# A Mamba-2 mixer with a ternary FFN: another order in the mixer's first ten steps and in step 64, and other turns for the side work of the FFN

## The chip, the cores and the metric

The kernel runs on one core of a Trainium2 chip, in one launch. The metric is the device time of the launch in microseconds (us). TensorE (PE), VectorE (DVE), ScalarE (ACT), GpSimd (POOL) and SyncE (SP) each run their own instructions in the order in which the program gives them; they wait for each other through semaphores. SP and POOL issue the transfers (DMAs).

## The reference

T = 4 x 256 = 1024 rows of 512 values. After a layer norm they go two ways: through a gated FFN with ternary weights, and through a Mamba-2 mixer (128 heads of 64, 8 groups, state 128). The output is x + mixer x silu(FFN). Cut to what matters:

```python
xn = layernorm(x)                                   # (4, 256, 512)
# mixer
zxbcdt = xn @ in_proj_w.T                           # gate 8192 | x 8192, B 1024, C 1024 | dt 128
xBC = silu(causal_conv(xBC, conv_w, 4 taps) + conv_b)
dt = softplus(dt + dt_bias);  Adt = -exp(A_log) * dt
# per head, with B, C shared by 16 heads, i >= j:
y[i] = sum_j (C[i] . B[j]) * exp(sum_{j<k<=i} Adt[k]) * dt[j] * x[j] + D * x[i]
# (the reference sums this in chunks of 32 with states)
y = y * silu(gate)
y = y * rsqrt(mean over group of y^2 + eps) * norm_w
s = y @ out_proj_w.T                                # 8192 -> 512
# FFN
hidden = silu(xn @ gate_w.T) * (xn @ up_w.T)        # 512 -> 1792, weights -1, 0, 1 times a scale
g = silu(hidden @ down_w.T)
return x + s * g
```

## The kernel before

**Two stages and an end.** `front` computes the layer norm and the FFN, and beside it what the mixer needs: dt and the decay rows, the B and C projections and the scores C.B of the 8 groups. Then the mixer runs in CT = 64 steps of 128 channels (two heads), and two more, 64 and 65, in which only older work is finished. At the end the last group's out-projection is done batch by batch (4 batches) and joined with the FFN's result.

**Products in seven parts.** Both projections of the mixer are done with 7 block products instead of 8 (a Strassen-like form). `product` (L173) issues two matmuls of a 128 x 128 block of weights by 512 columns. The weights are used as blocks a11, a12, a22 and as sums s1, s2, s3, s4, the activations as x11, x21, x22 and t1 to t4. `combine_w` (L142 to L146) makes the sums of weights on DVE, four additions a step. For the first EARLY = 7 steps the sums are made beside the FFN (`early_pieces`), stored to DRAM and loaded in the step. `out_first` (L701) is the same form of the out-projection, with its left sums (L681 to L684) and 7 products P0 to P6 of four matmuls; behind each product `leave` (L756) scales a result on ACT into `sa` or `sb`, which POOL's transfers (L889, L890, L892) add to `acc` in DRAM. The pool of sa and sb has one buffer each.

**FFN steps.** There are 28 (2 halves by 14 tiles). Each has a gate product, an up product, the down product of the step before, and three turns, in which `pieces` (84 turns and more) does its side work: `first_pieces` (the layer norm of tiles 4 to 7 and the activations' sums), from turn 5 on `dt_pieces` (thirteen pieces, two turns each, with exp and ln on ACT), at turns 11 + 8g `bc_pieces(g)` (the B and C projections of a group: products, three taps on DVE at L181, the last tap on ACT at L177, silu at L186, scores at L438), and from turn 26 on the sums for the mixer's first steps. The gate's silu is L520, the rounding rest of the hidden values is `hl` (L545). Copies of products to `cpad` and `xpad` are L404.

**A mixer step i.** The projection's seven products give the gate `gT` and the channels `xpad`; conv and silu give `xT`. In the same step the channels of i - 1 are worked on: the decay matrices m (two heads; rows broadcast from DRAM, `decay_scan` L592 on DVE, `decay_exp` L595 on ACT) are multiplied by the group's scores (`meet`, L598 and L599 on DVE), xT is transposed on PE (L604) and multiplied by dt into `v` (`values_0` L612 for the first block, `values_1` L621 for the second), and `y_products` (L645) sums y in PSUM (begun by `y_begin`, L631 on ACT). Channels i - 2 are gated in `y_gate` (L652) and written to DRAM; their squares are added to `sqacc` (L863, a transfer of POOL). From step 10 on each step also does 4 or 3 products of the out-projection of a group finished earlier.

**What sets the order.** The schedule is manual: each engine runs the instructions as the Python code emits them. For i < LEAD = 6 the silu of step i is put off to step i + 1, with the first exp behind it; from LEAD on both stand at the end of step i. The lines of a step that the change touches:

```python
                product(px, a11, x11, True)
                nc.scalar.copy(pz, px)                          # L782
            if old and i - 1 < LEAD:
                conv_silu(i - 1, xTs[i - 1])
                decay_exp(ms[i - 1][0])
            if old:
                decay_exp(ms[i - 1][1])
            if here:
                product(pq, s1, t1, True)
                product(px, s2, t2, False)
                nc.scalar.copy(gT[:, HALF:], px)                # L791
```

In step 64 nothing is projected (`here` is false). It gates channels 62, treats channels 63, and does P0 to P3 of an out-projection, P4 to P6 of which follow in step 65.

Of the kernel before, what the change touches and what calls it, by code (L numbers as in the profile page):

```python
# [61 lines left out]
G = 8  # L62
# [12 lines left out]
LEAD = 6  # L75
EARLY = 7
# [5 lines left out]
def mixer_ffn(ctx: ExitStack, tc: tile.TileContext, x, in_w, conv_w, conv_b, dt_bias, a_log, d_col,  # L82
# [23 lines left out]
    scp = main.enter_context(tc.tile_pool(name="scp", bufs=1))  # L106
# [82 lines left out]
    def front(pre, one_of, fp, f2, hp, wq):  # L189
# [136 lines left out]
        def dt_ln():  # L326
            nc.scalar.activation(ln, u, AF.Ln)
            nc.vector.scalar_tensor_tensor(e, u, 1.0, e, ALU.subtract, ALU.subtract)
            nc.scalar.activation(u, ln, AF.Exp, scale=-1.0)
# [43 lines left out]
        def first_pieces():  # L373
            yield
            for t in range(4, NT):
                keep(t, ln_tile(t))
                yield
            for n in range(4):
                combine_x(n)
                if n == 2:  # L380
                    held["a"] = combine_w(held.pop("w"))
                yield

        def dt_pieces():
            for piece in (lambda: dt_project(0), lambda: dt_project(1), dt_exp, dt_ln, dt_softplus,
                          dt_adt, dt_sums, dt_rows, lambda: transpose_heads(dt[:, 0], dth, 0),
                          lambda: transpose_heads(dt[:, 1], dth, 1),
                          lambda: transpose_heads(adt0, adt, 0), tail_sums, tail):
                piece()
                yield  # L390
                yield

        def bc_pieces(g):
# [7 lines left out]
            for a, b, to in ((a11, x11, cpad_h[0]), (s2, t2, cpad_h[1]), (s3, t3, bpad_h[1]),  # L401
                             (a22, t4, bpad_h[0])):
                product(px, a, b, a is a11)
                nc.scalar.copy(to, by_batch(px))  # L404
                yield
# [15 lines left out]
            s = scp.tile([P, 3, KT // 2, P], F32, name="s")  # L421
            held["a"] = factors(w, s)
            sums = combine_to(s[:, 0], s[:, 1], s[:, 2], blocks(w)[2], w)
            next(sums)
            yield
            next(sums)
            conv_taps(i_b, bT, xpad, (0,))
            conv_silu(i_c, cT)
            yield
            conv_taps(i_b, bT, xpad, (1, 2))  # L430
# [16 lines left out]
        def early_pieces():  # L447
            for n in range(EARLY):
                w = wq.tile([P, 2, KT, P], F32, name="wq")
                for m, i in enumerate((n + 1, CT + n + 1)):  # L450
                    nc.sync.dma_start(w[:, m], in_w[i])
                for _ in range(4):
                    yield
                s = wq.tile([P, 4, KT // 2, P], F32, name="sq")
                yield from combine_to(s[:, 0], s[:, 1], s[:, 2], s[:, 3], w)
                nc.sync.dma_start(early[n], s)
                yield

        def all_pieces():

            turn, chains = 0, [first_pieces()]
            later = []
            while chains or later or turn < 11 + 8 * G:
                if turn == 5:
                    later.append(dt_pieces())
                if turn >= 11 and (turn - 11) % 8 == 0 and (turn - 11) // 8 < G:
                    chains.insert(0, bc_pieces((turn - 11) // 8))
                if turn == 26:
                    later.append(early_pieces())
                if turn > 11 and (turn - 11) % 8 == 4 and len(chains) > 1:  # L470
# [39 lines left out]
        for t in range(4, NT):  # L510
            ln_stats(t)
        ln_std(4, 4)
        nc.vector.reciprocal(rstd[:, 4:], rstd[:, 4:])
# [54 lines left out]
    yap = main.enter_context(tc.tile_pool(name="yap", bufs=2, reuse_waits="tile"))  # L568
# [172 lines left out]
    with tc.manual_schedule():  # L741
# [3 lines left out]
        sqacc, rs, ya, outs = None, None, None, None  # L745
        for i in range(CT + 2):
# [4 lines left out]
            sums = []  # L751
# [5 lines left out]

            if i + 1 <= EARLY:
# [24 lines left out]
            if old and i - 1 < LEAD:  # L783
                conv_silu(i - 1, xTs[i - 1])
                decay_exp(ms[i - 1][0])
            if old:
                decay_exp(ms[i - 1][1])
            if here:
                product(pq, s1, t1, True)
                product(px, s2, t2, False)  # L790
                nc.scalar.copy(gT[:, HALF:], px)  # L791
                if i:
                    decay_scan(ms[i][0])
# [24 lines left out]
            if og >= 0 and on % 2 == 0:  # L818
                ob, ya = on // 2, nxt
                left, sums = left_factors(ya)  # L820
                for make in sums:
                    make()
# [13 lines left out]
            if here:  # L836
                product(px, a22, t4, False)
                nc.scalar.copy(xpad_h[0], by_batch(px))
                product(pq, s4, x22, False)
                nc.vector.tensor_add(gT[:, HALF:], gT[:, HALF:], pq)  # L840
            if old:
# [6 lines left out]
            if og >= 0:  # L848
                if on % 2 == 0:
                    sa = osp.tile([P, NC, HID], F32, name="sa")  # L850
                    sb = osp.tile([P, 3, HH], F32, name="sb")
                    outs = out_first(left, rights[og], leave)
                for n in range(4 - on % 2):
                    next(outs)
                    if here and n == 1:
                        nc.scalar.activation(gT[:, HALF:], gT[:, HALF:], AF.Silu)
            elif here:
                nc.scalar.activation(gT[:, HALF:], gT[:, HALF:], AF.Silu)
# [7 lines left out]
            if here:  # L866
# [12 lines left out]
                if i == 0:  # L879
                    decay_scan(ms[i][0])  # L880
                decay_scan(ms[i][1])
# [13 lines left out]
            elif i == CT:  # L895
                nxt = load_gated(G - 1, 0, PER_G - 1)
# [20 lines left out]
        for b in range(NB):  # L917
# [14 lines left out]
            sums = []  # L932
            for n, _ in enumerate(out_first(left, rights[G - 1], leave_last)):
                if n == 4:
# [4 lines left out]
            if b + 1 < NB:  # L939
                left, sums = left_factors(yas[b + 1])  # L940
                for make in sums:
                    make()
# [50 lines left out]
```

## Time and profile before

| | |
|---|---|
| median of 3 runs | 1818.32 us (1817.26 to 1818.66) |
| profiled execution | 1815.84 us, of which the core's span is 1814.1 |
| mean granted clock of TensorE | 0.993 |
| a mixer step without out-projection, step 5 (410.55 to 428.33) | 17.78 us |
| a step with `combine_w`, step 8 (465.16 to 484.21) | 19.05 us |
| P0 of the four last batches starts | 1756.81, 1769.03, 1782.60, 1796.16 |

All times inside the kernel are microseconds from the start of the span, for one profiled execution. L12 is line 12 of the kernel before. In a line of the timeline the columns are start, duration, engine, line, operation, output and inputs, count, and in brackets the idle time of the engine before it, with what ended it. PEclk is the clock that TensorE was granted, 1.00 being full speed. Matmul ends are modelled, so that a busy PE is not PE at its peak.

### The profile page before, as it was taken

To read this page: it belongs to the slowest core of one execution; us is meant where nothing else is said; L and a number is where in the kernel's file an instruction comes from. 1 tells how busy PE (TensorE), PEld (TensorE's weight loads), DVE (VectorE), ACT (ScalarE), POOL (GpSimd) and SP (SyncE) were. 2 spreads that over 40 slices of the span, in tenths; PEclk is the share of its full clock that TensorE was granted. 3 is DMA by queue.
4 is the path that set the end of the run, shared out by engine and by line. 5 is a ranking of instruction groups with operands and counts; after the bars stand their busy time and mean duration, and the time that the engine had idled before them with its cause. 6 is when DMAs were issued, how large, how long until landed. Compare 5 with 4: busy or idle time off the path is not lost.

```text
span 1814.1 us, 22556 instructions
## 1 busy us (share of the span) xinstructions
PE 1744.4 (96%) x8494; PEld 1116.3 (62%) x8494; DVE 1448.0 (80%) x1739; ACT 1069.8 (59%) x1420; POOL 194.7 (11%) x235
## 2 busy tenths in 40 slices
PE   8999999899899999999999999999999999999988
PEld 6566666444456666666666666666666666666676
DVE  5557665689898888888888888888888888888866
ACT  3443333576666666666666666666666666666630
POOL 2212221000000000111011101110111011101110
PEclk9999999999999999999999999999999999999989
DMA  5134543557646665766676667665766676667665
GB/s 203 64 134 174 180 139 108 192 188 243 200 161 204 197 201 181 205 197 196 188 206 197 201 182 205 197 203 181 205 196 201 183 205 194 192 193 204 177 183 168
DMA packets 161739, 337.05 MB, mean 186 GB/s; under 512 B 15072, under 2 KB 54752, under 8 KB 161632
## 3 DMA queue, kind: packets, MB, share of 16 engines
q1 hardware_dynamic: 139120, 283.19, 44.7%
q0 software_dynamic: 22512, 52.44, 16.6%
q8 instruction: 67, 1.10, 0.2%
q14 instruction: 40, 0.33, 0.1%
HBM read 232.55 MB, written 74.19 MB: 169 GB/s over the span
## 4 chain that ended last, share of the span: by engine, by line
PE 85%; DVE 6%; ACT 5%; DMA 1%; issue 1%; SPq 0%; DVEq 0%; ACTq 0%
PE px L173 27%; PE po L701 21%; PE pq L173 13%; PE py L645 9%; PE pz L173 6%; PE pp L283 4%; PE pf L291 2%; ACT xpad L803 2%; PE tp L604 1%; PE pg L438 1%; DMA wd_i<-in_down_t 1%; ACT m L595 1%; PE pv L663 1%; DVE xT L181 1%; DVE cT L181 1%
## 5 line engine op out<-in xcount | busy, mean ns | idle before, releaser
L173 PE MATMUL px<-xc,w 128*128 128x512 f32 x576 | 280.1, 609 | 26.3 <-ACT xpad L803 15.7
L592 DVE TENSOR_TENSOR_SCAN m<-m,after 128x1024 f32<-128x1024 f32 x128 | 291.8, 2281 | 0.0
L181 DVE SCALAR_TENSOR_TENSOR xT<-xpad,cw,xT 128x1024 f32<-128x1024 f32 x192 | 246.1, 1282 | 4.6
L173 PEld LDWEIGHTS px<-xc,w 128*128 128x128 f32 x576 | 103.8, 190 | 147.1 <-issue 97.2
L701 PE MATMUL po<-wo,ya 128*128 128x256 f32 x768 | 178.1, 382 | 0.0
L645 PE MATMUL py<-m,v 128*64 128x128 f32 x2048 | 160.6, 276 | 5.3 <-DVE v L621 5.3
L598 DVE TENSOR_TENSOR m<-m,gm 128x1024 f32<-128x1024 f32 x128 | 154.7, 1209 | 6.8 <-ACT m L595 6.8
L701 PEld LDWEIGHTS po<-wo,ya 128*128 128x128 f32 x768 | 142.6, 192 | 17.4 <-issue 0.2
L863 POOL DMA_DIRECT2D sqacc<-sq x55 | 48.3, 878 | 955.0 <-ACT sq L815 955.0
L173 PE MATMUL px<-xc,s 128*128 128x512 f32 x288 | 136.0, 594 | 6.6 <-ACT pz L782 6.3
L173 PE MATMUL px<-xnT,w 128*128 128x512 f32 x288 | 141.8, 614 | 0.0
L173 PE MATMUL pq<-xc,s 128*128 128x512 f32 x288 | 135.4, 592 | 1.4 <-DMA s<-early 1.4
L173 PE MATMUL pq<-xnT,s 128*128 128x512 f32 x288 | 135.7, 593 | 0.5 <-DVE xpad L827 0.4
L595 ACT ACTIVATE m<-m 128x1024 f32<-128x1024 f32 x128 | 134.8, 1057 | 1.7 <-DVE m L592 0.9
L173 PE MATMUL pz<-xnT,w 128*128 128x512 f32 x288 | 135.3, 592 | 0.0
L645 PEld LDWEIGHTS py<-m,v 128*64 128x64 f32 x2048 | 116.9, 137 | 27.3 <-issue 19.8
L701 PE MATMUL po<-tw,sy 128*128 128x256 f32 x512 | 116.9, 380 | 2.8 <-DVE sy L681 1.5
L840 DVE TENSOR_TENSOR gT<-gT,pq 128x512 f32<-128x512 f32 x64 | 43.9, 687 | 83.5 <-PE pq L173 83.5
L604 PEld LDWEIGHTS tp<-ident,xT 128*128 128x128 f32 x512 | 64.1, 141 | 74.9 <-issue 74.9
L827 DVE TENSOR_TENSOR xpad<-xpad,pq 128x512 f32<-128x512 f32 x64 | 43.8, 684 | 83.3 <-ACT xpad L803 83.1
L701 PEld LDWEIGHTS po<-tw,sy 128*128 128x128 f32 x512 | 96.8, 190 | 18.4 <-DVE m L922 2.8
L652 DVE TENSOR_TENSOR yg<-py,gT 128x512 f32<-128x512 f32 x128 | 83.8, 678 | 27.6 <-PE py L645 27.6
(168 smaller groups left out, 3072.3 us busy)
## 6 DMA issues: line engine op xcount, KB each, us to landing
m<-rows SPq DMA_DIRECT2D x128, 512.0 KB, 6.1
w<-in_in_w SPq DMA_DIRECT2D x137, 256.0 KB, 6.6
mo<-rows SPq DMA_DIRECT2D x128, 256.0 KB, 7.0
gated<-yg SPq DMA_DIRECT2D x64, 512.0 KB, 8.2
ya<-gated SPq DMA_DIRECT2D x31, 1024.0 KB, 7.0
sqacc<-sq POOLq DMA_DIRECT2D x55, 512.0 KB, 5.4
wo<-in_out_w SPq DMA_DIRECT2D x64, 256.0 KB, 6.9
acc<-sa POOLq DMA_DIRECT2D x24, 512.0 KB, 5.9
```

The lines of the kernel that those rows point to most:

```text
L173: nc.tensor.matmul(pp, a[:, k, :], b[:, k, :], start=start and k == 0, stop=k == KT // 2 - 1, skip_group_check=not start)
L181: nc.vector.scalar_tensor_tensor(xT, xpad[:, :, k:k + L], cw[:, i, k:k + 1], xT, ALU.mult, ALU.add)
L283: nc.tensor.matmul(pp, w[:, k * P:(k + 1) * P], part[:, k, :], start=(k == 0 and part is xh), stop=(k == KT - 1 and part is xl))
L592: nc.vector.tensor_tensor_scan(m, m, after, 0.0, ALU.add, ALU.mult)
L595: nc.scalar.activation(m, m, AF.Exp)
L598: nc.vector.tensor_mul(m, m, gm[:, 0:T])
L604: nc.tensor.transpose(tp[:, b, :], xT[:, b, c * P:(c + 1) * P], ident)
L645: nc.tensor.matmul(py[d, q * P:(q + 1) * P], v[:, b, h, :], m, start=False, stop=stop, skip_group_check=True)
L652: nc.vector.tensor_mul(yg[:, 2 * i:2 * i + 2, :], ps[i], by_batch(gT[:, i * HALF:(i + 1) * HALF]))
L701: nc.tensor.matmul(po, a[:, k, :], b[:, k, :], start=start and k == 0, stop=k == HG - 1, skip_group_check=not start)
L840: nc.vector.tensor_add(gT[:, HALF:], gT[:, HALF:], pq)
L863: nc.gpsimd.dma_start(sqacc, sq, accum_op=ALU.add)
```

## The change

- LEAD becomes 9 and EARLY 11. For steps 8 to 11 the sums of weights are thus made beside the FFN too, and loaded.
- Beside the FFN: statistics of tiles 4 to 7 move from before the first FFN step into the first turns; the pieces of dt get turn counts of their own, start a turn later, and the inverse is split off; the sums of the next group's weights stand behind products s2 and s3; the B taps are a turn earlier; the early sums start at turn 20 and take five turns each instead of seven.
- In the first steps of the mixer the second exp stands behind the gT copy (in step 1 there is no exp), the values of block 1 ahead of the gT addition on DVE as long as there is no out-projection, and step 0 ends with both exps.
- In step 64 and 65 the left sums and the products of the out-projection open the step.
- Batches 0 and 1 of the last group are loaded in step 64; in the last stage the left sums of batch b + 1 are made one by one from the fourth product of batch b on.
- Pools `scp` and `yap` get a buffer more each.

```diff
-LEAD = 6
-EARLY = 7
+LEAD = 9
+EARLY = 11
...
-    scp = main.enter_context(tc.tile_pool(name="scp", bufs=1))
+    scp = main.enter_context(tc.tile_pool(name="scp", bufs=2))
...
             nc.vector.scalar_tensor_tensor(e, u, 1.0, e, ALU.subtract, ALU.subtract)
+
+        def dt_inverse():
             nc.scalar.activation(u, ln, AF.Exp, scale=-1.0)
...
         def first_pieces():
+            for t in range(4, NT):
+                ln_stats(t)
+                if t % 2:
+                    yield
+            ln_std(4, 4)
+            nc.vector.reciprocal(rstd[:, 4:], rstd[:, 4:])
             yield
...
-            for piece in (lambda: dt_project(0), lambda: dt_project(1), dt_exp, dt_ln, dt_softplus,
-                          dt_adt, dt_sums, dt_rows, lambda: transpose_heads(dt[:, 0], dth, 0),
-                          lambda: transpose_heads(dt[:, 1], dth, 1),
-                          lambda: transpose_heads(adt0, adt, 0), tail_sums, tail):
+            for piece, turns in ((lambda: dt_project(0), 2), (lambda: dt_project(1), 1),
+                                 (dt_exp, 3), (dt_ln, 3), (dt_inverse, 1), (dt_softplus, 1),
+                                 (dt_adt, 2), (dt_sums, 2), (dt_rows, 1),
+                                 (lambda: transpose_heads(dt[:, 0], dth, 0), 1),
+                                 (lambda: transpose_heads(dt[:, 1], dth, 1), 1),
+                                 (lambda: transpose_heads(adt0, adt, 0), 1), (tail_sums, 2),
+                                 (tail, 1)):
                 piece()
-                yield
-                yield
+                for _ in range(turns):
+                    yield
...
                 nc.scalar.copy(to, by_batch(px))
+                if a is s2:
+                    s = scp.tile([P, 3, KT // 2, P], F32, name="s")
+                    held["a"] = factors(w, s)
+                    sums = combine_to(s[:, 0], s[:, 1], s[:, 2], blocks(w)[2], w)
+                if a is not a11:
+                    next(sums, None)
                 yield
...
             conv_taps(i_c, cT, cpad, (2,))
-            s = scp.tile([P, 3, KT // 2, P], F32, name="s")
-            held["a"] = factors(w, s)
-            sums = combine_to(s[:, 0], s[:, 1], s[:, 2], blocks(w)[2], w)
-            next(sums)
+            conv_taps(i_b, bT, xpad, (0,))
             yield
-            next(sums)
-            conv_taps(i_b, bT, xpad, (0,))
             conv_silu(i_c, cT)
+            conv_taps(i_b, bT, xpad, (1, 2))
             yield
-            conv_taps(i_b, bT, xpad, (1, 2))
             yield
...
-                for _ in range(4):
+                for _ in range(2):
                     yield
...
-                if turn == 5:
+                if turn == 6:
                     later.append(dt_pieces())
...
-                if turn == 26:
+                if turn == 20:
                     later.append(early_pieces())
...
-    yap = main.enter_context(tc.tile_pool(name="yap", bufs=2, reuse_waits="tile"))
+    yap = main.enter_context(tc.tile_pool(name="yap", bufs=3, reuse_waits="tile"))
...
+            if not here:
+                left_sums()
+                project_out(lambda: None)
...
-            if old and i - 1 < LEAD:
+            lead = old and i - 1 < LEAD
+            if lead:
                 conv_silu(i - 1, xTs[i - 1])
-                decay_exp(ms[i - 1][0])
-            if old:
+                if i > 1:
+                    decay_exp(ms[i - 1][0])
+            elif old:
                 decay_exp(ms[i - 1][1])
             if here:
                 product(pq, s1, t1, True)
                 product(px, s2, t2, False)
                 nc.scalar.copy(gT[:, HALF:], px)
+                if lead and i > 1:
+                    decay_exp(ms[i - 1][1])
...
                 nc.scalar.copy(xpad_h[0], by_batch(px))
+                if i == 0:
+                    decay_scan(ms[i][0])
+                    decay_scan(ms[i][1])
                 product(pq, s4, x22, False)
+            if old and og < 0:
+                vs.append(values_1(i - 1, xTs[i - 1]))
+            if here:
                 nc.vector.tensor_add(gT[:, HALF:], gT[:, HALF:], pq)
-            if old:
+            if old and og >= 0:
                 vs.append(values_1(i - 1, xTs[i - 1]))
...
-                if i == 0:
-                    decay_scan(ms[i][0])
-                decay_scan(ms[i][1])
+                if i:
+                    decay_scan(ms[i][1])
+                else:
+                    decay_exp(ms[i][0])
+                    decay_exp(ms[i][1])
...
-                nxt = load_gated(G - 1, 0, PER_G - 1)
+                yas = {b: load_gated(G - 1, b, PER_G - 1) for b in range(2)}
...
-        yas = {0: nxt, 1: load_gated(G - 1, 1)}
-        last = yas[0][:, PER_G - 1, :]
-        nc.vector.tensor_copy(last, yg[:, 0, :])
+        yas[2] = load_gated(G - 1, 2)
+        for b in range(2):
+            nc.vector.tensor_copy(yas[b][:, PER_G - 1, :], yg[:, b, :])
...
             for n, _ in enumerate(out_first(left, rights[G - 1], leave_last)):
+                if n == 3 and b + 1 < NB:
+                    ahead, sums = left_factors(yas[b + 1])
+                if n >= 3 and b + 1 < NB:
+                    sums.pop(0)()
...
-            if b + 1 < NB:
-                left, sums = left_factors(yas[b + 1])
-                for make in sums:
-                    make()
+            left = ahead
             if b + 2 < NB:
-                yas[b + 2] = load_gated(G - 1, b + 2)
                 whole[b + 2] = fetch(b + 2)
+            if b + 3 < NB:
+                yas[b + 3] = load_gated(G - 1, b + 3)
```

`left_sums` and `project_out` hold the lines that made the left sums and called `out_first` before, unchanged; in steps 0 to 63 they are called at the old places.

More of the change, by code (lines that the diff above doesn't have):

```diff
@@ L509, in front @@
             keep(t, tps[t])
[L510 to L513, printed above, removed]
         last = None
@@ L744, in mixer_ffn @@
         xTs, gTs, yps, wos, rights, toms = {}, {}, {}, {}, {}, {}
-        sqacc, rs, ya, outs = None, None, None, None
+        sqacc = rs = ya = outs = left = nxt = ob = sa = sb = None
         for i in range(CT + 2):
@@ L750, in mixer_ffn @@
             wg, wn = og + 1, on
-            sums = []
             def leave(po, row, col, layer):
@@ L756, in leave, with project_out, left_sums @@
                 nc.scalar.mul(to, po, rs[:, 2 * ob + row:2 * ob + row + 1])
+            def project_out(between):
+                nonlocal sa, sb, outs
+                if on % 2 == 0:
+                    sa = osp.tile([P, NC, HID], F32, name="sa")
+                    sb = osp.tile([P, 3, HH], F32, name="sb")
+                    outs = out_first(left, rights[og], leave)
+                for n in range(4 - on % 2):
+                    next(outs)
+                    if n == 1:
+                        between()
+            def left_sums():
+                nonlocal ob, ya, left
+                if og >= 0 and on % 2 == 0:
+                    ob, ya = on // 2, nxt
+                    left, sums = left_factors(ya)
+                    for make in sums:
+                        make()
+            if not here:
+                left_sums()
+                project_out(lambda: None)
             if i + 1 <= EARLY:
@@ L815, in mixer_ffn @@
                     nc.scalar.activation(sq, yf, AF.Square)
-            if og >= 0 and on % 2 == 0:
-                ob, ya = on // 2, nxt
-                left, sums = left_factors(ya)
-                for make in sums:
-                    make()
+            if here:
+                left_sums()
             if wg >= 0 and wn == PER_G - 1:
@@ L838, in mixer_ffn @@
                 nc.scalar.copy(xpad_h[0], by_batch(px))
+                if i == 0:
+                    decay_scan(ms[i][0])
+                    decay_scan(ms[i][1])
                 product(pq, s4, x22, False)
+            if old and og < 0:
+                vs.append(values_1(i - 1, xTs[i - 1]))
+            if here:
                 nc.vector.tensor_add(gT[:, HALF:], gT[:, HALF:], pq)
-            if old:
+            if old and og >= 0:
                 vs.append(values_1(i - 1, xTs[i - 1]))
@@ L847, in mixer_ffn @@
                 nc.scalar.activation(gT[:, 0:HALF], pz, AF.Silu)
[L848 to L858, printed above, removed]
+                if og >= 0:
+                    project_out(lambda: nc.scalar.activation(gT[:, HALF:], gT[:, HALF:], AF.Silu))
+                else:
+                    nc.scalar.activation(gT[:, HALF:], gT[:, HALF:], AF.Silu)
             if old:
@@ L878, in mixer_ffn @@
                     ms[i + 1] = load_rows(i + 1)
-                if i == 0:
-                    decay_scan(ms[i][0])
-                decay_scan(ms[i][1])
+                if i:
+                    decay_scan(ms[i][1])
+                else:
+                    decay_exp(ms[i][0])
+                    decay_exp(ms[i][1])
             if here and i >= LEAD:
@@ L930, in end @@
                 nc.sync.dma_start(out[t * P:(t + 1) * P, cols], to)
-            sums = []
             for n, _ in enumerate(out_first(left, rights[G - 1], leave_last)):
+                if n == 3 and b + 1 < NB:
+                    ahead, sums = left_factors(yas[b + 1])
+                if n >= 3 and b + 1 < NB:
+                    sums.pop(0)()
                 if n == 4:
@@ L938, in mixer_ffn @@
             end(1, slice(0, HH))
-            if b + 1 < NB:
-                left, sums = left_factors(yas[b + 1])
-                for make in sums:
-                    make()
+            left = ahead
             if b + 2 < NB:
-                yas[b + 2] = load_gated(G - 1, b + 2)
                 whole[b + 2] = fetch(b + 2)
+            if b + 3 < NB:
+                yas[b + 3] = load_gated(G - 1, b + 3)
     main.close()
```

## The prediction

> **What bounds the kernel now.** I read the page's busy line first, then TensorE's table of waits, then the timeline around the long waits, and last the granted clock where they end.
>
> ```profile
> PE 1744.4 (96%) x8494; PEld 1116.3 (62%) x8494; DVE 1448.0 (80%) x1739; ACT 1069.8 (59%) x1420; POOL 194.7 (11%) x235
> PE   8999999899899999999999999999999999999988
> ```
>
> TensorE (PE) is busy 1744.4 of 1814.1 us, so at most 70 us can be won by a new order, and the change removes no matmul. These 70 us, by releaser (microseconds in all, times, longest):
>
> ```profile
> PE px L173 <- ACT xpad L803: 15.7, 64, 0.7
> PE tp L604 <- DVE v L612: 8.2, 1, 8.2
> PE tp L257 <- DVE xt L252: 6.8, 4, 3.2
> PE px L173 <- ACT pz L782: 6.3, 4, 1.6
> PE py L645 <- DVE v L621: 5.3, 9, 0.7
> PE px L173 <- ACT cpad L404: 5.3, 3, 3.3
> PE px L173 <- ACT gT L791: 3.8, 6, 2.0
> ```
>
> The xpad wait (0.24 us in each of 64 steps) stays. The others lie where the change works: L257, L404 beside the FFN, L791 in steps 1 to 6, L782 in steps 7 to 10, L621 in steps 1 to 9, L612 in step 64. A wait costs more than itself when the clock falls (timeline, idle time in brackets):
>
> ```profile
> 59.96 3.78 PE L173 MATMUL px<-xc,w 128*128 128x512 f32 x4 [3.27 <-ACT cpad L404]
> 307.43 1.51 PE L438 MATMUL pg<-cT,bT 128*128 128x128 f32 x8 [3.01 <-ACT bT L186]
> 346.59 1.98 PE L173 MATMUL px<-xc,w 128*128 128x512 f32 x4 [2.02 <-ACT gT L791]
> ```
>
> Behind the 3.27 gap four matmuls take 3.78 us, behind the 2.02 gap 1.98. In 2 us windows from each start the clock column is 0.50, 0.67 and 1.00. Work at reduced clock cost 2.75 us after the first and about 1.9 after the second (longer durations summed against the same shapes at full clock).
>
> **A, start of the FFN: +1.1 us** (plus is gain). LayerNorm statistics of tiles 4 to 7 leave VectorE's way ahead of FFN step 0. Replaying VectorE's order with its own durations, the two gaps of 3.19 and 1.46 become about 3.1 and 1.4; the same work is reached at 35.7 instead of 36.85. The moved statistics land in FFN turns 0 to 2, where VectorE is about half busy; without that cover they would delay the first hl by up to 1 us.
>
> **B, dt beside the FFN: +5.0.** The 3.27 wait came from ScalarE's run of tables:
>
> ```profile
> 54.00 1.06 ACT L327 ACTIVATE ln<-u 128x1024 f32<-128x1024 f32 x1
> 55.08 1.28 ACT L329 ACT_TABLE_LOAD   x1
> 56.37 1.06 ACT L329 ACTIVATE u<-ln 128x1024 f32<-128x1024 f32 x1
> 57.45 1.28 ACT L520 ACT_TABLE_LOAD   x1
> ```
>
> With the inverse at its own turn, cpad's copy no longer sits behind two table changes: 3.27 + 2.75 = 6.0 saved. Four more table loads come in all. A load is 1.28 us in these rows and the activation starts 0.01 behind it, so four are 5.1 us of an engine that is half idle there. The Trainium skill ("ScalarE: Activation LUTs", "What ACT_TABLE_LOAD costs") adds a drain of 1.38 us to each switch, 10.6 us for four; that speaks against the change and would halve this gain. The rows show no drain, so I take 1.28. Softplus, taps and adt fall into the same turns 16 and 17 on VectorE; hl is made there, and TensorE waits about 1.0 us more for it. Net +5.0, between +2 and +6.
>
> **C, rest of the FFN: +1, between -3 and +3.** The sums of the next group's weights move from two late turns to right behind products s2 and s3, and the B taps one turn up. The 3.01 gap becomes about 1.95 (one tap of 1.28 us less in front of the last silu) and then keeps the clock: up to +2.5. Against it: the weights are loaded at 78.45, 112.19, 141.20 and so on, land 4.6 to 5.8 us later, and the s2 products start at 87.64, 120.04, 149.47: slack of 1 to 4 us, below 2 for the third. Everything on VectorE behind a late load would wait (hl, and TensorE for it). EARLY's four more sums beside the FFN are 4 x 4 x 0.42 = 6.7 us of VectorE and 4 MB of transfers, both in idle time; they now wait two turns for their load instead of four. If that cover is gone, it is a wait of 1 to 2 us each.
>
> **D, steps 0 and 1: -1.5.** Both exps of m0 go to the end of step 0, a 1.28 us table load and 2 x 1.06 us, behind the scans. In the trace the scans of m0 ended at 345.0; the new place puts the first two ahead of the taps. ScalarE is then held until about 342.6, and pz's copy (L782) with it: TensorE waits 3.4 to 3.7 us there instead of 1.44 + 2.02 in two places, and the clock falls, which 2.02 did not make it do. -1.5, between -3 and +1.
>
> **E, steps 2 to 6: +3.2.** There the gT copy (L791) stood behind exp[1]: 0.36 us of wait a step. Copy first, and it is gone. Values of block 1 ahead of the gT add cut the v wait (L621) from 0.57 to about 0.3. 5 x 0.65 = 3.2. TensorE's own order in these steps is the same as before; only VectorE and ScalarE change.
>
> **F, steps 7 to 10: +5.4.** Windows of one step (length, then busy PE, PEld, DVE, ACT, POOL, clock):
>
> ```profile
> 410.55:428.33 17.78, 16.61 (x86) 8.64 (x84) 15.87 (x17) 12.88 (x16) 0.86 (x1) 1.00 0.74 235
> 465.16:484.21 19.05, 16.62 (x87) 8.61 (x85) 17.40 (x21) 13.03 (x16) 0.86 (x1) 1.00 0.69 214
> ```
>
> The second has VectorE's four additions for the next weights (4 x 0.42 us, 17.40 - 15.87 of busy time), and the silu of its own step in front of the pz copy, which TensorE awaits for 1.6 us. With EARLY 11 the additions give way to transfers (1 MB a step instead of 0.5 MB; DMA share is 0.69 to 0.74 in these windows), with LEAD 9 the silu moves on. Steps 7 and 8 become like step 6 less E's 0.65: 19.05 - 17.1 = 2.0 each. Step 9 saves 1.5, step 10 nothing: its table order is as before.
>
> **G, step 64: -10, between -11 and -6.** Before, the left sums and the products of the out-projection stood behind y_gate, meet and the transposes; TensorE idled 8.15 us. Now sums and P0 to P3 open the step. But `leave` writes sa and sb, of which there is one each, and step 63's are still being added to acc by POOL's queue:
>
> ```profile
> 1727.07 1.22 POOL L889 DMA_DIRECT2D acc<-sa  x1 [7.60 <-ACT sa L756]
> 1733.45 0.91 POOL L890 DMA_DIRECT2D acc<-sb  x1 [5.16 <-DMA acc<-sa]
> 1734.03 1.23 POOL L892 DMA_DIRECT2D acc<-sb  x1
> acc<-sb POOLq DMA_DIRECT2D x1, 128.0 KB, 7.9
> 1741.97 0.47 ACT L756 ACTIVATE sa<-po,rs 128x256 f32<-128x256 f32 x1 [8.27 <-PE po L701]
> 1743.70 0.47 ACT L756 ACTIVATE sb<-po,rs 128x256 f32<-128x256 f32 x1 [1.25 <-PE po L701]
> ```
>
> The last sb transfer lands at 1734.0 + 7.9 = 1741.9, so the old leaves never met it. The new ones do: leave 0 (sa) at 1733.3, leave 1 (sb) at 1741.9; P2 runs, P3 waits 6.9 us for its accumulator and runs at half clock to 1745.9. Queued behind these leaves on ScalarE are exp[1] (done 1747.6 instead of about 1734) and Square; behind exp[1] on VectorE meet and v (1.2 + 0.7 + 2 x 0.68, to 1750.7); behind v the transposes of block 1, a second gap of about 4.3, y_products (1755.7), and P4 to P6 of step 65 (1760.9); behind their leaves Square and the sqacc add at about 1762.7, which was 1753.08. For the clock, the skill ("TensorE: Matmul & The Clock Gate", "What's actually happening") halves it after an idle window of 3.4 us and restores it after 3.4 busy ones, which would be about 1.7 us of loss a gap, 3.4 in this step; this trace's rows show less regular drops (gaps of 3.01 and 3.27 sufficed) and 1.9 to 2.75 us each, about 4. I take 4.
>
> **H, last stage: +3.8.** Left sums of batch b+1 are made one a product from n = 3 on instead of four behind the batch. A batch is 13.57 us against 7 x 1.72 = 12.06 of products; the waits were
>
> ```profile
> PE po L701 <- DVE sy L681: 1.5, 3, 0.5
> PE po L701 <- DVE m L922: 1.4, 3, 0.5
> ```
>
> and P0 of the next batch repeated late. VectorE then has about 9.2 us a batch beside 12.06: hidden. 3 x 1.27. The load of batches 0 and 1 (two of 896 KB on SP in step 64 instead of one) ends before they are used in every reading below; the second copy of a last tile is 0.28 us of VectorE beside the wait for sqacc, and the larger pools cost nothing but space.
>
> **Sum.** 1.1 + 5.0 + 1.0 - 1.5 + 3.2 + 5.4 - 10 + 3.8 = +8.0 us. The profiled execution took 1815.84 (span 1814.1, 1.7 around it), 2.5 below the median of the runs; 8.0 less is 1807.8 for it, and 1818.3 - 8.0 = 1810.3 for the median.
>
> **Rivals.** (1) The sum holds: 1804 to 1814.5, chance 0.54. (2) The sb transfers do not bite: step 63's land before the new leaves need them, for instance because POOL's queue is earlier by then. Replayed without that wait, G is 0 to +1: 1800. For it: the sb transfer varies, 3.9 to 10.4 us. Against it: issue at 1734 is fixed by acc<-sa landing, which the change doesn't touch, and two loads of 896 KB now start near it. 0.2. (3) Given back beside the FFN: VectorE at turns 16 and 17 and the doubled table loads push hl back by 5 to 6 us: 1815.5, no change. 0.16. (4) Slower: the weight sums of the B/C pieces meet their load. The landing of w is 6.6 us over the whole run and 4.6 to 5.8 here; with six early pieces' loads on the same queue it may be 7 to 8. From a stall of 1.2 us in each of seven groups on, all the gain is gone; at 1.8 us each, 12.6 in all, the time is 1823; it is slower beyond the bound from about 1.7. 0.10. (5) That the change doesn't do what it says is partly so: "transposes of block 1 behind P3" changes TensorE's order in step 64 alone.
>
> **How the numbers follow.** A difference below 0.2% (3.6 us: 1814.7 to 1821.9) cannot be told from none. Cases 1 and 2 and a quarter of case 3 are faster (0.54 + 0.20 + 0.04), the rest of case 3 is within the bound, case 4 is slower: 0.78, 0.12, 0.10. The range reaches to case 2 below and over case 3 above: 1798 to 1818.
>
> **What would show it.** After: no gap over 2.5 us at cpad L404; PE's wait for pz L782 near 1.6 us in all; four DVE additions less in steps 7 to 10; in step 64 a leave idle "<-DMA acc<-sb" and P3 behind it; batches of 12.3 us at the end. Wrong if step 64's gap ends within 2 us of the new leaves' first products, if waits for hl exceed 6 us, or if VectorE waits for w in the FFN.

## The result, and the profile after

The changed kernel takes 1814.17 us (median of 20 runs, 1811.82 to 1818.41) against 1817.78 us before (20 runs, 1816.10 to 1818.68). The ratio is 0.9983, with a 95% interval from 0.9976 to 0.999: 3.6 us faster by the medians, clear of no change, but not of the 0.2% below which the prediction calls two times the same. Forecast were 8.0.

Three lines of the page after, to be set beside those of before:

```profile
PE 1751.6 (96%) x8494; PEld 1123.5 (62%) x8494; DVE 1448.0 (80%) x1740; ACT 1076.4 (59%) x1424; POOL 196.8 (11%) x235
PE   8999999999899999999999999999999999999969
PEclk9999999999999999999999999999999999999979
```

TensorE runs the same 8494 matmuls but is busy 7.2 us longer: more of them ran at a reduced clock (mean 0.987 instead of 0.993). The profiled execution took 1817.91 us, the third longest of the 20, and 2.1 us more than the profiled one of before. The times follow the clock: the three runs above 1817.9 us had a mean clock of 0.987, the six below 1813.1 had 0.990 or 0.991. So the trace is read for where time goes, the medians for how much.

TensorE's waits after, by releaser (microseconds in all, times, longest):

```profile
PE px L173 <- ACT xpad L838: 15.8, 64, 0.7
PE po L711 <- ACT sb L765: 6.9, 1, 6.9
PE tp L257 <- DVE xt L252: 6.8, 4, 3.3
PE px L173 <- ACT cpad L417: 4.4, 1, 4.4
PE tp L614 <- DVE v L622: 4.2, 1, 4.2
PE py L655 <- DVE v L631: 3.9, 10, 0.4
PE pv L673 <- DMA sqacc<-sq: 3.9, 1, 3.9
PE pv L673 <- DVE sqacc L896: 2.9, 1, 2.9
PE pf L291 <- DVE hl L555: 2.8, 2, 1.7
PE px L173 <- ACT pz L813: 2.5, 1, 2.5
```

Gone are the waits for gT (3.8), most of those for pz (6.3 to 2.5), the one of 8.2 for v in step 64, and those for sy and m in the last stage. New are sb, sqacc twice, and one of 4.4 for cpad, later than the old one of 3.3.

How far the profile after is ahead of the profile before, read at the start of the same piece of work in each (negative: behind). A row of a single profile can be off by a low clock in it that another run of the same code doesn't have: e10 below has the FFN of before unchanged, and its profile is 1.2 us ahead of that of before in the middle of it.

| point | lead, us | since the row above |
|---|---|---|
| down product of the third FFN step (47.6 before) | 1.0 | part A, +1.0 |
| FFN at 122 us | 7.5 | part B, +6.5 |
| FFN at 193 | 3.8 | C: cpad wait at 179.5, -3.7 |
| end of the FFN | 7.0 | C: shorter wait for bT at 302, +3.2 |
| step 2 | 6.5 | D, -0.5 |
| step 7 | 9.0 | E, +2.6 (0.52 a step) |
| step 9 | 12.6 | F, +3.6 (17.27 us a step, before 19.05) |
| step 11 | 7.8 | steps 9 and 10, -4.8 |
| step 63 | 7.8 | nothing in 52 steps |
| last norm_sums | -2.6 | G, with that wait, -10.4 |
| P0 of batch 1 | -5.9 | low clock behind the wait for sqacc's last sum, -3.3 |
| end of P6, batch 3 | -1.5 | H, +4.4 (12.1 us a batch) |

The step of F, read in windows as in the prediction (step 8 after):

```profile
454.34:471.61 17.27, 16.62 (x87) 8.65 (x85) 15.88 (x17) 13.00 (x16) 0.86 (x1) 1.00 0.67 218
```

**Step 64** went as replayed. ScalarE's timeline after:

```profile
1725.50 0.47 ACT L765 ACTIVATE sa<-po,rs 128x256 f32<-128x256 f32 x1 [3.36 <-DMA acc<-sa]
1734.42 0.47 ACT L765 ACTIVATE sb<-po,rs 128x256 f32<-128x256 f32 x1 [8.45 <-DMA acc<-sb]
1739.03 1.05 ACT L605 ACTIVATE m<-m 128x1024 f32<-128x1024 f32 x1
```

and TensorE's:

```profile
1734.95 3.67 PE L711 MATMUL po<-wo,sy 128*128 128x256 f32 x8 [6.93 <-ACT sb L765]
1743.28 1.09 PE L614 MATMUL tp<-ident,xT 128*128 128x128 f32 x4 [4.22 <-DVE v L622]
```

The second leave waits 8.45 us for step 63's transfer; P3 waits 6.93 behind it and takes 3.67 us for eight matmuls that take 1.89 at full clock; the exp of the second head starts only at 1739.03, and the transposes wait 4.22 us for what follows from it.

**Step 10** holds what the prediction did not have:

```profile
493.95 3.54 PE L673 MATMUL pv<-one,sqacc 128*128 128x1 f32 x16 [3.86 <-DMA sqacc<-sq]
```

norm_sums needs the sum of squares in DRAM. In windows of 2 us from there on (length, busy PE, PEld, DVE, ACT, POOL, clock, share of DMA, GB/s) the clock stays at half for 8 us:

```profile
494.00:496.00 2.00, 2.00 (x10) 2.00 (x10) 2.00 (x4) 1.97 (x3) 0.00 (x0) 0.50 1.04 375
496.00:498.00 2.00, 2.00 (x8) 1.83 (x9) 2.00 (x2) 0.96 (x2) 0.00 (x0) 0.50 1.06 327
498.00:500.00 2.00, 2.00 (x3) 0.67 (x2) 1.13 (x2) 0.00 (x0) 0.00 (x0) 0.50 0.98 369
500.00:502.00 2.00, 2.00 (x4) 0.92 (x3) 0.00 (x0) 0.78 (x2) 0.00 (x0) 0.50 0.38 154
```

The transfer was issued at 482.33 and landed 11.5 us later. What was issued from 482.16 to 483.2, after (KB, microseconds to landing):

```profile
ya<-gated SPq DMA_DIRECT2D x1, 1024.0 KB, 6.1
sqacc<-sq POOLq DMA_DIRECT2D x1, 512.0 KB, 11.5
m<-rows SPq DMA_DIRECT2D x1, 512.0 KB, 11.2
s<-early SPq DMA_DIRECT2D x1, 384.0 KB, 8.6
```

Before, the same transfer was issued 3.7 us behind the megabyte of ya and landed in 5.6 us. After, all four start within 1.1 us, and SP's queue shows why (its waits, after):

```profile
SPq L682 <- DMA gated<-yg: 4.9, 1, 4.9
```

The load of ya waits there for the store of `gated` to land, and the early sums and the load of m stand behind it. That store took 5.3 us to land instead of 2.6, in a stretch that has the loads of the early sums besides, so ya went out 0.17 us ahead of the sum of squares instead of 3.7.

### The profile page after: what moved, and what is told of

It reads as the page before. It is cut to its first block, busy times and chain, and to the rows that moved or that the text cites. A ratio compares the mean times of both kernels' runs of the same rounds, so it can differ in the third digit from the quotient of the medians.

```text
span 1815.9 us, 22579 instructions
## 1 busy us (share of the span) xinstructions
PE 1751.6 (96%) x8494; PEld 1123.5 (62%) x8494; DVE 1448.0 (80%) x1740; ACT 1076.4 (59%) x1424; POOL 196.8 (11%) x235
## 4 chain that ended last, share of the span: by engine, by line
PE 90%; ACT 3%; DVE 3%; DMA 2%; issue 1%; SPq 0%; POOL 0%; DVEq 0%; ACTq 0%
PE px L173 28%; PE po L711 21%; PE pq L173 13%; PE py L655 9%; PE pz L173 7%; PE pp L283 5%; PE pf L291 2%; ACT xpad L838 2%; PE tp L614 2%; PE pg L452 1%; PE pv L673 1%; DMA sqacc<-sq 1%; DVE cT L181 1%; DMA acc<-sb 0%; PE pd L315 0%
## 5 line engine op out<-in xcount | busy, mean ns | idle before, releaser
L894 POOL DMA_DIRECT2D sqacc<-sq x55 | 47.6, 865 | 965.5 <-ACT sq L850 965.5
L765 ACT ACTIVATE sb<-po,rs 128x256 f32<-128x256 f32 x84 | 39.9, 475 | 114.5 <-PE po L711 106.0
```

The lines of the kernel that those rows point to most:

```text
L894: nc.gpsimd.dma_start(sqacc, sq, accum_op=ALU.add)
```

## The experiments

**e1: steps 64 and 65 in the old order.**

```diff
-            if not here:
-                left_sums()
-                project_out(lambda: None)
...
-            if here:
-                left_sums()
+            left_sums()
...
-                if og >= 0:
-                    project_out(...)
+            if og >= 0:
+                project_out(...)
```

> The changed kernel with the left sums and the products of the out-projection back at their old places in steps 64 and 65. Theory (waiting leaves): in the profile after, step 64 lost 10.4 us up to the end of norm_sums and 2.75 more by a low clock behind it. Both go: TensorE has one gap of about 8 us there again, no wait for acc<-sb, none for sqacc, and the last batches keep 12.1 us each. 11 to 13 us faster than the changed kernel: 1801 to 1804. Rival (the order of step 64 costs little, the step would lose the time somewhere else): 1811 or more.

1803.59 us, ratio to before 0.9918 (0.9905 to 0.9932), 10.6 below the changed kernel. Its waits have the old gap and neither sb nor the sum of squares at the end:

```profile
PE tp L614 <- DVE v L622: 8.2, 1, 8.2
PE pv L673 <- DMA sqacc<-sq: 3.8, 1, 3.8
```

Undoing this part wins what G was forecast to lose; the rival falls. The two profiles are 13.0 us apart from step 63 to P0 of batch 1; the medians give 10.6.

**e2: the new order, leaves into free buffers.**

```diff
+                    if here:
                         sa = osp.tile([P, NC, HID], F32, name="sa")
                         sb = osp.tile([P, 3, HH], F32, name="sb")
+                    else:
+                        sa = wp.tile([P, 2, KT, P], F32, name="w")
+                        sa = sa.rearrange("p m k i -> p m (k i)")
+                        sb = scp.tile([P, 3, KT // 2, P], F32, name="s")
+                        sb = sb.rearrange("p m k i -> p m (k i)")
```

> The changed kernel with its new order of steps 64 and 65, but the two results that the leaves write there lie in buffers of the weights and of their sums, which are free by then, so that no leave waits for a transfer of step 63. Theory (the transfers, not the order, cost the time): leaves without a wait for DMA, no gap of 6.9 us; step 64 and 65 as long as before the change or up to 2 us shorter, norm_sums without a wait: 1801 to 1804. Rival (the order itself costs: exp of the second head and Square queued behind leaves): at most 4 us faster than the changed kernel, 1810 or more.

1802.41 us, ratio 0.9922 (0.991 to 0.9935). The first two leaves no longer wait for a transfer (timeline of ScalarE):

```profile
1721.14 0.47 ACT L765 ACTIVATE w<-po,rs 128x256 f32<-128x256 f32 x1 [0.82 <-PE po L711]
1722.86 0.47 ACT L765 ACTIVATE s<-po,rs 128x256 f32<-128x256 f32 x1 [1.25 <-PE po L711]
```

So it is the buffer's release by the transfer, not the order of the products, that cost the time. What the expectation had wrong: norm_sums still waits 2.86 us, and v 4.22. With these the new order cannot be told from the old one (e1).

**e3: norm_sums behind the product with s3**, in each of the seven steps that have it (one call moved).

> The changed kernel with norm_sums behind the product with s3 instead of at the head of the step, in the seven steps that have it. In the profile after, step 10 waited 3.86 us there for the sum of squares in DRAM and ran at a clock of 0.5 until 503. Theory (a late transfer, and then the clock): wait and low clock both go, 6 to 8.5 us faster than the changed kernel, 1806 to 1808. Rival (transfers are simply too many in step 9 and what is late moves on to the next wait): a new wait in step 10 or 11 and at most 3 us faster.

1816.57 us (13 runs), ratio 0.9992 (0.9984 to 1.0001): no gain. In its profile the wait for the squares is gone, and its lead at step 11 is 12.6 instead of 7.8. But the transposes then wait for the Sqrt in each of seven steps:

```profile
1410.68 0.66 PE L614 MATMUL tp<-ident,xT 128*128 128x128 f32 x4 [0.58 <-ACT sd L676]
```

Five of the steps lose about 0.2 us by it and this one, step 50, 1.9, since the clock fell to 0.50 after 0.58 us of waiting behind sixteen one-column matmuls; it fell in step 10 too. This profile is that of the shortest of the 13 runs (1812.98). More such falls in the others would explain the median, but only this one has a trace. The theory of a late transfer was not tested well by this kernel; e6 does it.

**e4: the taps of B back at their old turns.**

```diff
-            conv_taps(i_b, bT, xpad, (0,))
             yield
+            conv_taps(i_b, bT, xpad, (0,))
             conv_silu(i_c, cT)
-            conv_taps(i_b, bT, xpad, (1, 2))
             yield
+            conv_taps(i_b, bT, xpad, (1, 2))
             yield
```

> The changed kernel with the taps of B at their old turns. Theory (the two taps moved up stand on VectorE ahead of the FFN's output at its half, ScalarE's copy to cpad is queued behind that): the wait of 4.37 us at 179.5 goes back below 2.5 us without a low clock, about 3.5 us won there; the wait for bT at about 302 goes back from 1.4 to 3.0 us with a low clock, about 3 us lost: in sum within 1.5 us of the changed kernel. Rival (the early sums, which fall into the same turn, are the cause): still more than 3 us of wait at 179, and 3 us slower than the changed kernel.

1819.26 us, ratio 1.001 (1.000 to 1.002): 5 us slower than the changed kernel. The cpad wait at 180 fell from 4.37 to 1.75 without a low clock, as the theory has it, and the wait for bT rose to 2.05. The rest of the expectation was wrong: new waits for xpad, 2.27 at 91 with a low clock and 1.16 at 126, took the lead from 6.5 to 0.3. In this kernel the sums behind s2 and s3 thus pay only with the taps' new turns.

**e5: e2, and exp and Square ahead of the leaves.**

```diff
             if not here:
                 left_sums()
-                project_out(lambda: None)
+                if old:
+                    decay_exp(ms[i - 1][1])
+                    project_out(lambda: None)
...
+            if i > CT:
+                square()
+                project_out(lambda: None)
```

> As e2 (step 64 and 65 in the new order, leaves into free buffers), and in step 64 the exp of the second head stands ahead of the leaves on ScalarE, in step 65 the gate and its Square ahead of the leaves of P4 to P6. e2 still had 4.22 us of idle TensorE for v and 2.86 for sqacc there, each with a low clock behind it. Theory (what was queued behind the leaves cost that): both waits fall below 1 us and the low clock at 1730 and at 1746 goes, 8 to 11 us faster than e2: 1791 to 1795. Rival (the chain meet, v, transposes is as long whatever stands ahead of it): less than 3 us faster than e2, 1799 or more.

1797.93 us, ratio 0.9889 (0.9876 to 0.9903), 4.5 below e2. The wait for v went from 4.22 to 1.47, that for sqacc went altogether. Less than forecast: in its profile the clock still fell to 0.56 at 1732 after the 1.47. The chain through exp, meet and v is shorter, not hidden. In size the result lies between theory and rival; the two waits answer to the theory.

**e6: the load of ya behind the loads of m, in step 9 alone.**

```diff
-                if r == 1 and i >= PER_G and here:
+                if r == 1 and i > PER_G + 1 and here:
                     nxt = load_gated((i - PER_G) // PER_G, 0)
...
                 if i + 1 < CT:
                     ms[i + 1] = load_rows(i + 1)
+                if i == PER_G + 1:
+                    nxt = load_gated((i - PER_G) // PER_G, 0)
```

> The changed kernel, with the load of the first gated megabyte (ya) in step 9 moved behind that step's loads of m, so that it no longer starts together with the transfer that adds the squares. Theory (that transfer landed in 11.5 us instead of 5.6 because it shared the queues with ya): it lands in 5 to 7 us, the wait of 3.86 us at norm_sums and the low clock up to 503 go, 6 to 8 us faster than the changed kernel in its profile, median 1806 to 1809. Rival (the loads of early sums and of m are what it shares the queues with): it still lands in 9 us or more and the wait stays above 2 us; within 2 us of the changed kernel.

1811.84 us, ratio 0.9965 (0.9952 to 0.9977), 2.3 below the changed kernel. The transfer lands in 4.5 us, and norm_sums does not wait. The transfer's line among the issues, and norm_sums in TensorE's timeline:

```profile
sqacc<-sq POOLq DMA_DIRECT2D x1, 512.0 KB, 4.5
```

```profile
490.18 1.95 PE L673 MATMUL pv<-one,sqacc 128*128 128x1 f32 x16
```

Lead at step 11: 13.6 instead of 7.8. The gain in the profile is 5.8; the median moved 2.3, less than half of it, and why is not shown beyond the low clock in the changed kernel's profiled execution. The edit moves more than ya: in SP's queue the early sums and the load of m no longer stand behind it and start 5 us earlier, at 477.38 and 477.86 instead of 482.58 and 483.20.

```profile
477.38 0.42 SPq L904 DMA_DIRECT2D s<-early  x1
```

So the run shows that starting all four together makes the transfer late, not which of the three others does it.

**e7: the FFN's output of the first half behind the third turn.** The calls `ffn_out(h - 1, done, (0,))`, `(1,)` and `(2, 3)` become one, `ffn_out(h - 1, done)`, at the last one's place.

> The changed kernel with the FFN's output tiles of the first half all written behind the third turn of the step, so that ScalarE's copy to cpad no longer stands behind them. Theory (the copy waited on ScalarE for the output's multiplication on VectorE, and that for the taps of B and early sums): no wait for cpad at 179.5, no low clock there, 4 to 6 us faster than the changed kernel: 1808 to 1810. Rival (VectorE is late in these turns anyway): the wait turns up at hl or at the next product within that step, less than 2 us faster.

1812.62 us, ratio 0.9976 (0.9965 to 0.9987), 1.6 below the changed kernel with intervals that overlap. The cpad wait is gone, but a wait comes back at the next product of the same FFN step: ScalarE now has four output tiles in front of the copy to xpad, and it sits idle for 4.08 us until VectorE, busy without a gap from 171.9 to 182.6 with taps, sums and hl, gives it the first of them (L299). In size and place this is the rival, and in part in cause. TensorE's timeline:

```profile
183.67 3.68 PE L173 MATMUL px<-xc,w 128*128 128x512 f32 x4 [3.53 <-ACT xpad L417]
```

**e8: e5, e6 and e7 together.**

> The edits of e5, e6 and e7 together. They lie in different stages, so gains should add: e5's time less 10 to 14 us, 1779 to 1784. If the stages interact through the phase of the clock or through the transfers, up to 4 us less.

1792.01 us, ratio 0.9861 (0.9848 to 0.9875). That is 5.9 below e5; the medians of e6 and e7 gave 2.3 and 1.6. The gains are not lost when put together; the forecast of 10 to 14, made with the profile's sizes, was too large, even with the 4 us allowed off.

**e9: LEAD = 6, EARLY = 7 in the changed kernel.**

> The changed kernel with LEAD = 6 and EARLY = 7 again. Theory (the gain of steps 7 to 9 was given back by the late transfer of squares at step 10): steps 7 and 8 take about 18.5 us each again instead of 17.3, step 9 too, together 4 to 5 us lost, and norm_sums in step 10 doesn't wait, 4 to 9 us won with its clock: within 3 us of the changed kernel, 1811 to 1817. Rival (the late transfer has nothing to do with it): norm_sums still waits over 2 us, and it is 4 us or more slower than the changed kernel: 1818 or more.

1813.19 us, ratio 0.9978 (0.9969 to 0.9987): the same as the changed kernel within the noise. Steps 7 to 10 wait 1.7 to 2.2 us for pz again, the sum of squares is issued 3.8 us behind ya and lands in 5.2 us, and norm_sums does not wait:

```profile
sqacc<-sq POOLq DMA_DIRECT2D x1, 512.0 KB, 5.2
```

So the late transfer takes both, the shorter steps with their early sums and ya at its old place in SP's queue; either changed (e9, e6) cures it. By the medians LEAD and EARLY won nothing in the changed kernel. With the transfer cured (e6 against e9) they win 1.35 us, where the traces put steps 7 to 10 of e6 7.7 us ahead of those of e9. The trace of e9 makes up for it elsewhere, with fewer low clocks before step 7 and a shorter wait for sb in step 64 (4.8 against 6.9); which of this is typical stays open.

**e10: the last stage's edits alone, on the kernel before** (the loads of ya ahead, `yap` with three buffers, one sum a product).

> The kernel before with the last stage's edits alone: loads of the last group's tiles ahead, left sums of batch b + 1 one by one from the fourth product of batch b on. Theory (the waits for sy and m at each batch's start go): batches of 12.1 us instead of 13.57, 4 to 4.5 us faster than before: 1813.3 to 1813.8. Rival (VectorE's sums delay the releases of the accumulators within the batch): 2 us or less.

1812.79 us, ratio 0.9975 (0.9965 to 0.9985): 4.6 us faster than before (1817.38 in that comparison), and no wait for sy or m is left. Part H by itself won as much as the whole change, by the medians 1.4 us more.

**e11: e8, with the output tiles 2 and 3 one FFN step later.**

```diff
             if f == 0 and h:
-                ffn_out(h - 1, done)
+                ffn_out(h - 1, done, (0, 1))
...
+            if f == 1 and h:
+                ffn_out(h - 1, done, (2, 3))
```

> As e8, with the third and fourth output tile of the FFN's first half one FFN step later, so that the copy to xpad does not stand behind all four of them. e8 still had 3.53 us of wait for xpad at 182.6, with a low clock. Theory (the queue on ScalarE): wait below 1.5 us, no low clock, 3 to 5 us faster than e8: 1787 to 1789. Rival (VectorE's taps and sums are the limit of these turns): the wait moves to hl or to a product in the next step, less than 2 us faster.

1790.03 us, ratio 0.9848 (0.9835 to 0.9862), 2.0 below e8 with intervals that overlap. The wait went from 3.53 to 2.33 with a low clock still behind it, so half of the theory's gain at most. This is the lowest median of the study, 27 us below the one before; e8 and e12 cannot be told from it. Its waits:

```profile
PE px L173 <- ACT xpad L859: 15.8, 64, 0.7
PE tp L257 <- DVE xt L252: 6.6, 4, 3.4
PE px L173 <- ACT pz L830: 4.5, 2, 2.5
PE po L710 <- ACT w L764: 2.6, 1, 2.6
PE px L173 <- ACT xpad L417: 2.3, 1, 2.3
PE tp L613 <- DVE v L621: 1.5, 1, 1.5
```

**e12: e11, with the second exp of step 0 in step 1.**

```diff
                 else:
                     decay_exp(ms[i][0])
-                    decay_exp(ms[i][1])
...
-                if lead and i > 1:
+                if lead:
                     decay_exp(ms[i - 1][1])
```

> As e11, with the second exp of step 0 in step 1 behind the gT copy, as in the later steps. The wait for pz in step 1 was 2.47 us in every profile, with a low clock in about half of them. Theory: the wait falls to about 1.4 us and the clock stays, 1 to 2.5 us faster than e11. Rival (two more table loads put the same time back at the next wait of step 1): no difference from e11, or slower by up to 1 us.

1790.65 us, ratio 0.9856 (0.9842 to 0.9869): no difference from e11. The pz wait fell from 2.47 to 1.51, and one of 1.16 for xpad took its place in the same step: the rival.

## Why the prediction was wrong, point by point

The sign and the mechanism of most parts were right, the size of the whole was not: 3.6 us where 8.0 were forecast. The step that failed is F: it was to win 5.4 us, and by the medians it won nothing (e9). By the medians, without G the changed kernel wins 1817.7 - 1803.6 = 14.1 us (e1); the prediction's other parts sum to 18.0. The 3.9 missing are of the size that e6 (2.3, step 10) and e7 (1.6, cpad at 179.5, not clear of noise) took back; that these sum to 3.9 is luck, since each is known to about 2 us only and part of F's loss was made good by other parts. G costs 10.6, forecast 10.

- **A**, forecast +1.1, measured +1.0, by luck as close as that: the gaps became 3.33 and 1.46, not 3.1 and 1.4, and eleven later profiles with the same start have -1.0 to +1.4 at this point.
- **B**, forecast +5.0, measured +6.5, of which 1.2 is luck: the profile before had a longer low clock at 60 than e10's with the same FFN. The further wait of 1.0 us for hl did not come: at 78.4 it is 1.13, before 0.97. The four more table loads cost TensorE nothing that the trace shows; after one at 61.61 of 1.28 us the silu starts at 62.91, so the choice of the row stands.
- **C**, forecast +1, measured -0.5: +3.2 at bT as forecast, but -3.7 at 179.5. There the FFN changes halves and its output is scaled on VectorE (L299), and ScalarE's cpad copy is queued behind that. The taps moved up (2.59 us) and an early sum came ahead of L299. The prediction looked for late loads of w in this part; VectorE's waits show none for w. It did not ask what else stands behind the taps in the one turn that differs from all others. Rival 4 is therefore out.
- **D**, forecast -1.5, measured -0.5 with a low clock, and +1.2 in e1's profile without one. The wait is 2.47, not 3.4 to 3.7.
- **E**, forecast +3.2, measured +2.6: 0.52 a step instead of 0.65, since the wait for v fell only to 0.41, not to about 0.3.
- **F** is the step that failed: forecast +5.4, measured -1.2 in the trace from step 7 to step 11 (+3.6, then -4.8) and nothing in medians (e9). The additions' going was sized well (1.78 a step instead of 2.0, and with the late transfer cured, in e6, steps 7 to 10 win 4.7 in the trace). What failed is the term for the transfers, which the sum put at nothing because the share of DMA was 0.69 to 0.74, and "step 10 nothing". It did not follow what step 9 has and step 5 doesn't: the first ya, and a sum of squares that the head of step 10 awaits. With the added loads the store of `gated` landed late (5.3 us; 2.6 before and in e9), so that ya, the early sums and m went out together with the sum of squares; this landed in 11.5 us instead of 5.6, and norm_sums waited 3.86 us, with 10 us of half clock.
- **G**, forecast -10, measured -10.4 to the last norm_sums and 10.6 in medians, by the mechanism forecast (waits of 6.93 and 4.22, forecast 6.9 and 4.3). Rival 2 is out. Of the clock, the prediction counted two gaps; a third one, the 2.86 us ahead of the last norm_sums, cost 3.3 us more behind it in the trace.
- **H**, forecast +3.8, measured +4.4 in the trace and 4.6 alone (e10).

For the clock, the prediction set a rule of 3.4 us of idle time and 3.4 us of recovery against the trace's rows. The runs decide for the rows, and the traces together say what sets them: see the last section.

## What to carry to other kernels

When a step gets shorter, list what the next step awaits at its head, transfers first, and ask what now starts together with each, and what stands behind a waiting load in the same queue: a mean share of DMA of 0.7 hides a moment in which four transfers, 2.4 MB, start within 1.1 us. Work that is moved to the head of a step needs buffers that the transfers of the step before have let go; e2 shows that a free buffer of another pool with the same shape is enough. And price a gap on TensorE by its wait and by the clock behind it, as a range: the same gap has both prices in different runs, so that medians decide over one profile.

## What the runs showed of the hardware

The same wait does not always cost the same. The wait for pz in step 1 is 2.47 us, within 0.1, in eleven profiles with the new step 0. In five of them (the changed kernel, e2, e5, e6, e11) the clock fell behind it, in six (e1, e3, e4, e7, e8, e9) it did not. The traces show what tells them apart. In each, the granted clock changes only at points that lie whole multiples of 3.41 us apart, and where these points fall differs from run to run. Two such windows in a row, of the changed kernel,

```profile
332.09:335.50 3.41, 0.94 (x4) 0.12 (x2) 3.34 (x4) 3.38 (x5) 0.00 (x0) 1.00 1.06 385
335.50:338.92 3.42, 3.42 (x4) 1.48 (x5) 3.42 (x4) 2.37 (x2) 0.00 (x0) 0.50 0.36 144
```

and of e7:

```profile
330.58:333.99 3.41, 1.91 (x4) 0.60 (x4) 3.34 (x3) 3.39 (x4) 0.00 (x0) 1.00 1.04 382
333.99:337.40 3.41, 2.45 (x6) 1.25 (x7) 3.41 (x3) 3.38 (x5) 0.00 (x0) 1.00 0.81 314
```

In the changed kernel the wait lies in one window, which leaves TensorE 0.94 us of work in it, and the next window is at half. In e7 it is split over two, with 1.91 and 2.45 us of work, and the clock stays. So with all eleven: the emptiest window around the wait was busy for 28 to 39% in the five, for 41 to 61% in the six. Over all fourteen traces (7163 windows at full clock behind the first 30 us) all 54 windows with at most 40% of busy time were followed by half clock; of the 11 between, 5 were; from 49% on it was three of 7098. The way back: of the windows at half clock, all 30 that were busy for less than 80% were followed by half again; of those from 90% on, 50 were followed by full clock and 11 by half. So a gap needs no idle window: 1.47 us with another of 0.41 behind it was enough in e8 (clock 0.50 from 1722 on), and the 1.6 us of each pz wait in the profile before never were. The Trainium skill ("TensorE: Matmul & The Clock Gate", "What's actually happening") has the clock set by a free-running window of 3.4 us, idle or busy. The window agrees with these traces; that it must be idle does not, and the measurement decides. The shares are of the profile's busy time, whose matmul ends are modelled, and no run set the phase on purpose.

One-column matmuls count as little or no work for it. The three windows from 49% on that were followed by half clock are all of e3 and have 1.6 to 1.9 us of them; one of those windows, with 2.83 us of busy time, 1.71 of them norm_sums, and the next:

```profile
1408.39:1411.80 3.41, 2.83 (x23) 2.50 (x22) 2.32 (x4) 3.08 (x4) 0.00 (x0) 1.00 1.09 315
1411.80:1415.21 3.41, 3.41 (x5) 1.35 (x4) 2.06 (x4) 0.98 (x2) 0.00 (x0) 0.50 0.23 46
```

And the 11 busy windows at half clock that were followed by half again are just those with 1 us or more of such matmuls. So norm_sums behind its wait in step 10 kept the clock at 0.50 for three windows (492.5 to 502.8), where behind the longer cpad wait at 179.5 it took two. Whether it is the single column or the load of weights for each that leaves the time uncounted was not tested.
